# The copy of the last scan states of a chunk, issued on GpSimd instead of ScalarE

## The chip, the cores and the metric

The kernel runs on one core of a Trainium2 chip. The metric is the device time of one execution in microseconds (us); lower is better. Five engines work side by side on a core, each with an instruction queue that it works through in order: TensorE (PE, its weight loads shown apart as PEld), VectorE (DVE), ScalarE (ACT), GpSimd (POOL) and the DMA queue of SyncE (SP).

## The reference, cut to what matters

The input is x, 8 sequences of 1024 tokens with 256 features. The model is a "macaron" layer: half a feed-forward block, a Mamba block, half a feed-forward block, each added to x.

```python
x = x + 0.5 * ffn(layernorm(x))          # fp4 quantise and dequantise, 704 hidden features
x = x + mamba(layernorm(x))              # 512 inner channels, 16 states a channel
x = x + 0.5 * ffn(layernorm(x))

# inside mamba
dA  = jnp.exp(delta[..., None] * A)
dBu = delta[..., None] * Bm[:, :, None, :] * u[..., None]
def step(h, inp):
    dA_t, dBu_t, c_t = inp
    h = dA_t * h + dBu_t
    return h, jnp.einsum('bdn,bn->bd', h, c_t)
```

The part that the change touches is the scan: h runs along the 1024 tokens of a sequence, for each of 512 channels and 16 states, and each h is multiplied by C of its token and summed over the 16 states.

## The kernel before, in words

The tokens are cut into 16 chunks of 512; a sequence is two chunks, so every odd chunk continues an even one. Counting from 0, the even chunks 0, 2, ... 14 begin a sequence and the odd ones end it. Each chunk passes five stages: the first feed-forward block (`stage_f1`), the front of Mamba (`stage_m1`: norm, projections, convolution, delta), the gate (`stage_z`), the scan (`scan`), and the output with the second feed-forward block (`stage_out`). While one chunk is scanned, the feed-forward work of its neighbours is woven in, so all engines always have work of several stages.

The scan of a chunk runs over 16 states k. For each k, `scan_step` makes four tiles s_bu (L874, ACT: delta times u times B, 128 tokens by 512 channels), and then, for each of four groups dc of 128 channels: s_da = exp(delta A) (L878, ACT), four transposes of s_bu into a PSUM tile s_pb (L881, PE; two such buffers), and the scan along the 512 tokens (L883, DVE), which writes a quarter of the tile s_h (five buffers, shared with other tiles of that size). s_h is laid out as two halves a, each of 512 tokens by two channel groups. In an even chunk L908 then copies the last token's 4 values a partition into s_carry, which the odd chunk's scans of the same k read as their initial value, 16 states and some 140 us later. `times_c` (L888) multiplies s_h in place by C, in two products of 1024 elements a partition on POOL. Because it works in place, the first product has to come after the copy of L908 has read s_h. At last the product is added into DRAM by a DMA with an adding write, issued by POOL (L920), or for k = 15 the two DRAM accumulators are added onto s_h (L914, L915), which `stage_out` takes up as y (L852, POOL).

POOL also does the products of the quantisation (`quant`, L543, L545, L552), the Mamba product of L803, and small products of the norm (L610, L613). ACT also does all copies out of PSUM, tanh, squares, the norm's scale and shift.

The order of instructions in each engine's queue is not the program's order. `set_order` (L386) builds a graph of all instructions, gives each a price (`price`, L141) and each pair of engines a lag (`LAG`, L99), plans a list schedule forward and backward in 70 passes, plays the 16 best with random delays, and fixes the winner's order on each engine by ordering dependencies. A small operation on ACT is priced at 93 ns and its elements at 1/1.2 ns each (L158); a copy on POOL falls to the last line of `price` (L177), 176 ns and 1 ns an element. When any instruction changes its engine or price, the whole plan is made anew and the order can move anywhere in the program.

`BE` (L42) chooses a share of the s_bu tiles for VectorE; with `BE = (0,)` the condition of L871 is never true, and all s_bu tiles are made at L874. `CE` (L43) is not used.

Of the kernel before, what the change touches and what calls it, by code (L numbers as in the profile page):

```python
# [14 lines left out]
AF = mybir.ActivationFunctionType  # L15
ALU = mybir.AluOpType
# [21 lines left out]
KS = 1  # L38
KE = 1
W_T = ((0.01, 0.08, 0.085), (0.02, 0.09, 0.095), (0.15, 0.25, 0.3), 0.2)  # L40

BE = (0,)  # L42
CE = (0,)  # L43
BUFS = {
    'accd': 4, 'bcol': 2, 'big': 1, 'bu': 7, 'carry': 2, 'cbc': 2, 'cd': 4, 'da': 4, 'delta': 2,
    'duT': 4, 'h': 5, 'h2': 4, 'hnT': 2, 'ht': 1, 'mv': 4, 'ncar': 2, 'qm': 2, 'qr': 3, 'qs': 4,
# [381 lines left out]
def macaron(ctx: ExitStack, tc: tile.TileContext, x_in, norm_w, norm_b, in_w, conv_w,  # L428
            conv_b, xp_w, dt_w, dt_b, a_log, d_par, out_w, w_gate, w_up, w_down, out):
    nc = tc.nc  # L430
    NB, L, _ = x_in.shape
    chunks = []
    for b in range(NB):
        t = 0
# [3 lines left out]
    S = len(chunks)  # L438
# [90 lines left out]
    def pairs(h, n):  # L529

        return h.rearrange("p (a t q) -> p a t q", a=ND // 2, q=2)[:, :, :n, :]
# [166 lines left out]
    duT, delta, bcol = {}, {}, {}  # L698
    carry = {}
# [132 lines left out]
    def load_y(s):  # L832
        y = pairs(sb.tile([P, ND * T], F32, tag="big", bufs=BUFS["big"], name="o_y"), chunks[s][2])
        yf = y.rearrange("p a t q -> p a (t q)")
        nc.sync.dma_start(yf, accd[s][0])
        nc.gpsimd.dma_start(yf, accd[s][1], accum_op=ALU.add)
        return y
# [25 lines left out]
    def scan_step(s, k, h):  # L863
        n = chunks[s][2]
        nt = n // P
        first = chunks[s][1] == 0
        bu_v = BE[S - 1 - s] if S - 1 - s < len(BE) else 0
        bu = []
        for t in range(nt):
            b = sb.tile([P, DI], F32, tag="bu", bufs=BUFS["bu"], name="s_bu")  # L870
            if t * bu_v % nt < bu_v:  # L871
                nc.vector.tensor_scalar(b, duT[s][t], bcol[s][:, t, k : k + 1], None, ALU.mult)
            else:
                nc.scalar.activation(b, duT[s][t], AF.Copy, scale=bcol[s][:, t, k : k + 1])  # L874
            bu.append(b)
        for dc in range(ND):
            da = sb.tile([P, T], F32, tag="da", bufs=BUFS["da"], name="s_da")[:, :n]
            nc.scalar.activation(da, delta[s][dc], AF.Exp, scale=an[:, dc, k : k + 1])  # L878
            pb = psb.tile([P, T], F32, tag="psb", name="s_pb")[:, :n]
            for t in range(nt):  # L880
                nc.tensor.transpose(pb[:, t * P : (t + 1) * P], bu[t][:, dc * P : (dc + 1) * P], ident)  # L881
            init = 0.0 if first else carry[chunks[s][0]][:, k, dc : dc + 1]
            nc.vector.tensor_tensor_scan(h[:, dc // 2, :, dc % 2], da, pb, init, ALU.mult, ALU.add)  # L883

    def times_c(s, k, h, cbc):
        last = s >= S - KE and k >= NS - 2
        for a in range(ND // 2):
            (nc.vector if last and a else nc.gpsimd).tensor_tensor(  # L888
                h[:, a], h[:, a], cbc.unsqueeze(2).to_broadcast([P, chunks[s][2], 2]), ALU.mult)

    def scan(s):
        n = chunks[s][2]
        if chunks[s][1] == 0:

            carry[chunks[s][0]] = sb.tile([P, NS, ND], F32, tag="carry", bufs=BUFS["carry"], name="s_carry")
        for k in range(0, NS, 2):
            cbc = sb.tile([P, 2, T], F32, tag="cbc", bufs=BUFS["cbc"], name="s_cbc")[:, :, :n]
            nc.sync.dma_start(cbc, cd[s][0:1, k * n : (k + 2) * n].rearrange("o (a t) -> o a t", a=2)
                              .partition_broadcast(P))
            if s >= S - KE and k == NS - 2:  # L900
                y_of[s] = load_y(s)
            last = s >= S - KE and k == NS - 2
            for j in range(2):
                h = pairs(sb.tile([P, ND * T], F32, tag="h", bufs=BUFS["h"], name="s_h"), n)
                hf = h.rearrange("p a t q -> p a (t q)")
                scan_step(s, k + j, h)
                if chunks[s][1] + n < L:
                    nc.scalar.activation(carry[chunks[s][0]][:, k + j].rearrange("p (a q) -> p a q", q=2), h[:, :, n - 1, :], AF.Copy)  # L908
                times_c(s, k + j, h, cbc[:, j, :])
                if last:  # L910
                    last_h.setdefault(s, []).append(h)
                elif k + j == NS - 1:

                    nc.gpsimd.dma_start(hf, accd[s][1], accum_op=ALU.add)  # L914
                    nc.gpsimd.dma_start(hf, accd[s][0], accum_op=ALU.add)  # L915
                    y_of[s] = h
                elif k + j == 1:
                    nc.sync.dma_start(accd[s][1], hf)
                else:
                    nc.gpsimd.dma_start(accd[s][j], hf, accum_op=ALU.add)  # L920
                yield
# [13 lines left out]
    for s in range(S):  # L935
        d = chunks[s][2] / T
        pf, pm = (16, 11) if d == 1 else (9, 9)
        f0 = FIRST[s][0] if s < len(FIRST) else t0 + T_F
        m0 = FIRST[s][1] if s < len(FIRST) else max(t0 + T_M, m1)
        m1 = t0 - E_M if s < len(FIRST) else m0 + d * (t0 - E_M - m0)  # L940
        spread(stage_f1(s), f0, min(f0 + d, m0), pf, K_F if s < KS else 0)
        spread(stage_m1(s), m0, m1, pm, K_M if s < KS else 2)
        spread(stage_z(s), t0 + T_Z, t0 + T_Z + 0.5 * d, ND, 3)
        spread(scan(s), t0, t0 + d, NS)
        t0 += d
        spread(stage_out(s), t0 + T_O, t0 + T_O + d, pf + 3, K_O if s >= S - KE else 1)
# [32 lines left out]
```

## Time and profile before

| | before |
|---|---|
| time of 3 runs, us | 2448.34, 2451.12, 2452.19 (median 2451.12) |
| profiled execution: its time | 2451.14 us |
| profiled execution: its span in the trace | 2449.0 us |
| mean granted TensorE clock | 0.99 |
| the first scan starts, that of chunk 15 starts | 149.5 us, 2261.7 us |
| L908 copies on ACT | 128, 25.9 us of recorded duration, 202 ns mean |

The page of the profile has the busy time of each engine over the span, the span in 40 slices, the DMA queues, the chain of work that ended last followed back from the last instruction, and the costliest groups of instructions with the idle time of the engine before them and what ended it. Other views of the same trace are used: the busy time in stretches of the span, here cut where the scan of a chunk starts, the list of waits (engine and line that waited, what released it, microseconds in total, times, longest), and the timeline of one engine. In the timeline a line has its start, its duration, engine, line of the kernel, operation, tiles out<-in, shape, and in brackets the idle time ahead of it and what ended it.

### The profile page before, as it was taken

How to read it: one execution, taken by the hardware profiler on the slowest of the kernel's cores; microseconds unless marked ns; L12 is line 12 of the kernel's file. 1: busy time of each engine (PE TensorE's matmuls, PEld its weight loads, DVE VectorE, ACT ScalarE, POOL GpSimd, SP SyncE). 2: the span in 40 equal slices, each digit the busy share in tenths (PEclk: the TensorE clock that was granted, in tenths of full speed). 3: DMA queues.
4: the chain of work that ended last, by engine and by line, in shares of the span. 5: the costliest groups of instructions: out<-in, count | busy, mean ns of one | idle time of the engine just before them, and what ended most of it. 6: DMA issues, size and time to landing. Idle time of an engine off the chain costs nothing.

```text
span 2449.0 us, 33713 instructions
## 1 busy us (share of the span) xinstructions
PE 2341.7 (96%) x11260; PEld 1617.9 (66%) x11260; DVE 2177.9 (89%) x3074; ACT 2142.2 (87%) x3952; POOL 2064.2 (84%) x1554
## 2 busy tenths in 40 slices
PE   7989999999999999999999999999999999998888
PEld 5566666667676666666667666666667666655556
DVE  7569898998989899898999889898998989888995
ACT  4489898999989998998999899898998999999852
POOL 4358898899989999898897999899898999888972
PEclk8999999999999999999999999999999999999899
DMA  3049888787877888598886978889787888899970
GB/s 94 18 115 192 192 166 197 166 200 170 165 191 168 203 185 187 138 185 193 175 196 140 210 169 171 189 173 208 167 178 174 179 190 191 189 211 199 198 149 18
DMA packets 90461, 416.28 MB, mean 170 GB/s; under 512 B 12016, under 2 KB 30320, under 8 KB 53552
## 3 DMA queue, kind: packets, MB, share of 16 engines
q0 software_dynamic: 36576, 266.35, 57.6%
q1 hardware_dynamic: 53712, 147.78, 18.4%
q8 instruction: 88, 1.44, 0.2%
q14 instruction: 85, 0.70, 0.1%
HBM read 129.42 MB, written 284.69 MB: 169 GB/s over the span
## 4 chain that ended last, share of the span: by engine, by line
PE 59%; ACT 13%; POOL 11%; DVE 8%; issue 4%; DMA 3%; SPq 0%; POOLq 0%; DVEq 0%; ACTq 0%
PE s_pb L881 11%; PE f_po L662 9%; PE f_pg L642 9%; PE f_pu L642 8%; PE m_pc L765 6%; POOL s_h L888 5%; DVE s_h L883 4%; ACT s_bu L874 4%; PE m_px L755 3%; ACT s_da L878 3%; PE m_pz L823 3%; PE o_po L857 2%; PE m_pp L775 2%; PE m_pd L791 2%; DMA s_h<-accd 2%
## 5 line engine op out<-in xcount | busy, mean ns | idle before, releaser
L888 POOL TENSOR_TENSOR s_h<-s_h,s_cbc 128x1024 f32<-128x1024 f32 x510 | 1136.9, 2270 | 125.0 <-ACT s_carry L908 71.0
L878 ACT ACTIVATE s_da<-m_delta,an 128x512 f32<-128x512 f32 x1024 | 720.7, 718 | 35.3 <-DVE s_h L883 33.5
L881 PEld LDWEIGHTS s_pb<-ident,s_bu 128*128 128x128 f32 x4096 | 505.3, 142 | 335.6 <-issue 132.5
L874 ACT ACTIVATE s_bu<-m_duT,m_bc 128x512 f32<-128x512 f32 x1024 | 701.4, 717 | 12.5 <-PE s_pb L881 9.9
L881 PE MATMUL s_pb<-ident,s_bu 128*128 128x128 f32 x4096 | 652.3, 277 | 44.7 <-DVE s_h L883 34.4
L883 DVE TENSOR_TENSOR_SCAN s_h<-s_da,s_carry,s_pb 128x512 f32<-128x512 f32 x512 | 638.3, 1264 | 22.2 <-PE s_pb L881 18.9
L883 DVE TENSOR_TENSOR_SCAN s_h<-s_da,s_pb 128x512 f32<-128x512 f32 x512 | 608.5, 1206 | 27.3 <-PE s_pb L881 20.2
L662 PE MATMUL f_po<-wdn,f_ht 128*128 128x256 f32 x1536 | 395.3, 382 | 10.0 <-ACT f_ht L659 7.8
L642 PE MATMUL f_pg<-wg,f_xt 128*128 128x352 f32 x1024 | 365.4, 465 | 4.4 <-ACT f_xt L632 1.8
L642 PE MATMUL f_pu<-wu,f_xt 128*128 128x352 f32 x1024 | 360.3, 463 | 5.2 <-DVE f_h L646 3.2
L662 PEld LDWEIGHTS f_po<-wdn,f_ht 128*128 128x128 f32 x1536 | 270.0, 190 | 76.2 <-issue 22.7
L765 PE MATMUL m_pc<-m_xp,cdg 128*128 128x512 f32 x512 | 253.4, 596 | 1.9 <-ACT m_car L762 1.8
L552 POOL TENSOR_TENSOR f_h<-f_h,q_sc 128x704 f32<-128x704 f32 x128 | 195.9, 1534 | 50.8 <-DVE f_h L551 46.2
L642 PEld LDWEIGHTS f_pu<-wu,f_xt 128*128 128x128 f32 x1024 | 177.6, 191 | 89.5 <-issue 21.7
L920 POOL DMA_DIRECT2D accd<-s_h x223 | 209.6, 940 | 26.3 <-POOL s_h L888 18.0
L642 PEld LDWEIGHTS f_pg<-wg,f_xt 128*128 128x128 f32 x1024 | 176.0, 191 | 80.7 <-issue 21.1
L545 POOL TENSOR_TENSOR f_h<-f_h,q_rc 128x704 f32<-128x704 f32 x120 | 176.5, 1479 | 17.0 <-DVE q_rc L544 10.3
L646 DVE SCALAR_TENSOR_TENSOR f_h<-f_h,f_pg 128x352 f32<-128x352 f32 x256 | 129.0, 505 | 37.6 <-ACT f_h L645 36.5
L645 ACT ACTIVATE f_h<-f_pg 128x352 f32<-128x352 f32 x256 | 116.9, 457 | 48.0 <-PE f_pg L642 47.5
L543 POOL TENSOR_SCALAR q_sc<-q_mx 128x44 f32<-128x44 f32 (+2 forms) x198 | 85.5, 439 | 74.2 <-DVE q_mx L542 66.8
L647 DVE TENSOR_TENSOR f_h<-f_h,f_pu 128x352 f32<-128x352 f32 x256 | 129.3, 506 | 18.7 <-PE f_pu L642 17.2
L755 PE MATMUL m_px<-m_hnT,inw 128*128 128x512 f32 x256 | 128.0, 606 | 3.0 <-DVE m_u L769 1.7
(114 smaller groups left out, 3384.6 us busy)
## 6 DMA issues: line engine op xcount, KB each, us to landing
accd<-s_h POOLq DMA_DIRECT2D x223, 1024.0 KB, 9.6
s_cbc<-cd SPq DMA_DIRECT2D x128, 512.0 KB, 6.0
s_h<-accd POOLq DMA_DIRECT2D x30, 1024.0 KB, 8.5
accd<-m_ud SPq DMA_DIRECT2D x16, 1024.0 KB, 13.1
accd<-s_h SPq DMA_DIRECT2D x16, 1024.0 KB, 5.8
x4a<-_attn_hidden_states_dram SPq DMA_DIRECT2D x16, 512.0 KB, 4.3
x1d<-x4a SPq DMA_DIRECT2D x16, 512.0 KB, 6.5
x4b<-x1d SPq DMA_DIRECT2D x16, 512.0 KB, 3.5
```

Source lines behind the costliest of these rows:

```text
L545: mul0.tensor_tensor(vb, vb, rc.unsqueeze(2).to_broadcast([P, g, BLK]), ALU.mult)
L552: mul1.tensor_tensor(vb, vb, sc.unsqueeze(2).to_broadcast([P, g, BLK]), ALU.mult)
L642: nc.tensor.matmul(dst, xt[:, c, :], w[:, c, hf * FH : (hf + 1) * FH], start=(c == 0), stop=(c == 1))
L662: nc.tensor.matmul(po, ht[:, k, :], wdn[:, k, :], start=(k == 0), stop=(k == NF - 1))
L755: nc.tensor.matmul(px, inw[:, c, dc * P : (dc + 1) * P], hnT[:, c, :n], start=(c == 0), stop=(c == 1))
L765: nc.tensor.matmul(pc, cdg[:, dc, k, :], xp[:, k : k + n], start=(k == 0), stop=(k == KC - 1))
L874: nc.scalar.activation(b, duT[s][t], AF.Copy, scale=bcol[s][:, t, k : k + 1])
L878: nc.scalar.activation(da, delta[s][dc], AF.Exp, scale=an[:, dc, k : k + 1])
L881: nc.tensor.transpose(pb[:, t * P : (t + 1) * P], bu[t][:, dc * P : (dc + 1) * P], ident)
L883: nc.vector.tensor_tensor_scan(h[:, dc // 2, :, dc % 2], da, pb, init, ALU.mult, ALU.add)
L888: (nc.vector if last and a else nc.gpsimd).tensor_tensor(h[:, a], h[:, a], cbc.unsqueeze(2).to_broadcast([P, chunks[s][2], 2]), ALU.mult)
L920: nc.gpsimd.dma_start(accd[s][j], hf, accum_op=ALU.add)
```

## The change

GpSimd now issues the copy of L908, as a `tensor_copy`, at the same place in the program: after the four scans of a state and ahead of the two products. The number of copies, their source and their destination are the same. The knobs `BE` and `CE` are removed, with the branch that `BE = (0,)` never took. The plan of all queues is made anew, with the copy priced as a POOL instruction.

```diff
-BE = (0,)
-CE = (0,)
...
-        bu_v = BE[S - 1 - s] if S - 1 - s < len(BE) else 0
         bu = []
         for t in range(nt):
             b = sb.tile([P, DI], F32, tag="bu", bufs=BUFS["bu"], name="s_bu")
-            if t * bu_v % nt < bu_v:
-                nc.vector.tensor_scalar(b, duT[s][t], bcol[s][:, t, k : k + 1], None, ALU.mult)
-            else:
-                nc.scalar.activation(b, duT[s][t], AF.Copy, scale=bcol[s][:, t, k : k + 1])
+            nc.scalar.activation(b, duT[s][t], AF.Copy, scale=bcol[s][:, t, k : k + 1])
             bu.append(b)
...
                 if chunks[s][1] + n < L:
-                    nc.scalar.activation(carry[chunks[s][0]][:, k + j].rearrange("p (a q) -> p a q", q=2), h[:, :, n - 1, :], AF.Copy)
+                    nc.gpsimd.tensor_copy(carry[chunks[s][0]][:, k + j].rearrange("p (a q) -> p a q", q=2), h[:, :, n - 1, :])
                 times_c(s, k + j, h, cbc[:, j, :])
```

## The prediction

> **What bounds the kernel now.** I read the page's busy shares first, then the stretches by chunk, then the waits. The stretches are cut where a chunk's scan starts (even chunks begin at 149.5, 427.8, 714.0, ...). The columns are the stretch, its length, and the busy time of PE, PEld, DVE, ACT and POOL with instruction counts, then granted clock, DMA share and GB/s.
>
> ```profile
> 149.50:278.90 129.40, 120.02 (x564) 78.82 (x562) 111.87 (x148) 123.16 (x232) 109.40 (x78) 0.96 0.87 191
> 278.90:427.80 148.90, 143.92 (x683) 99.43 (x683) 138.20 (x200) 133.41 (x240) 134.80 (x103) 0.98 0.83 178
> 427.80:569.20 141.40, 138.61 (x678) 96.81 (x678) 131.00 (x190) 132.05 (x250) 126.54 (x94) 1.00 0.81 180
> 714.00:851.50 137.50, 135.62 (x662) 93.94 (x661) 129.05 (x187) 128.81 (x247) 125.22 (x93) 1.00 0.80 180
> 1863.50:2000.60 137.10, 136.09 (x669) 95.72 (x668) 128.15 (x184) 130.31 (x250) 125.94 (x94) 1.00 0.81 184
> 2131.70:2261.70 130.00, 116.92 (x546) 76.00 (x546) 106.53 (x130) 120.93 (x223) 111.60 (x76) 0.99 0.92 205
> ```
>
> The reader is to see two kinds of stretch. In the middle (four of the lines) PE is busy for all but 1 to 5 us of 137 to 149; those stretches are PE's, and nothing in the change touches PE's work. In chunk 0 (first line) and chunk 14 (last line) PE idles 9.4 and 13.1 us, and ACT is the fullest engine (idle 6.2 and 9.1). These are where the copies on ACT could set the time. The head (0 to 149.5) and chunk 15 (2261.7 to the end) hold no copy.
>
> POOL idles 11 to 20 us in every stretch with copies, ACT 6 to 13. The waits say for what:
>
> ```profile
> PEld s_pb L881 <- DVE s_h L883: 95.8, 207, 1.8
> POOL s_h L888 <- ACT s_carry L908: 71.0, 53, 8.0
> ...
> POOL s_h L888 <- DVE s_h L883: 48.8, 67, 2.1
> ...
> PEld s_pb L881 <- ACT s_bu L874: 25.6, 51, 1.9
> ```
>
> POOL's longest wait is for the copy, 71.0 us in 53 pieces. But in the odd chunks, which have no copy, it waits for the scan itself (48.8 us in 67): most of the 71 us is the scan being awaited, under another name. And who waits for the products? In the list for line L888 only the DMA issue of L920 does (20.2 us, 59 times), never PE or DVE. A product earlier or later by half a microsecond reaches PE only through POOL's other work.
>
> **What the change removes: 128 copies on ACT.** Their rows show 202 ns each, 25.9 us. That is not what ACT gets back, since records overlap:
>
> ```profile
> 153.25 1.32 ACT L878 ACTIVATE s_da<-m_delta,an 128x512 f32<-128x512 f32 x2
> 154.48 0.19 ACT L908 ACTIVATE s_carry<-s_h 128x4 f32<-128x4 f32 x1
> 154.57 0.70 ACT L874 ACTIVATE s_bu<-m_duT,m_bc 128x512 f32<-128x512 f32 x1
> ```
>
> The next instruction starts 0.09 us after the copy; the median over the 114 copies with ACT busy on both sides is 95 ns. So ACT gets 128 x 0.095 = 12.2 us, 1.5 us an even chunk, plus the 2.6 us for which it stood waiting for a scan ahead of a copy.
>
> **What it adds: 128 copies on POOL.** The trace has no POOL copy. Bounds from the nearest rows: below, the 3-element MEMSET of L758, 40 ns (median end to end behind a busy POOL); above, the 32-element TENSOR_SCALAR of L543, 0.32 us. Nearest in shape and in reading two small operands from SBUF is L613 (128x4), behind its producer on POOL:
>
> ```profile
> 1310.06 1.03 POOL L610 TENSOR_TENSOR bn_y<-bn_ve,mhalf 128x4 f32<-128x4 f32 x1 [0.98 <-ACT bn_ve L609]
> 1311.17 0.20 POOL L613 TENSOR_TENSOR bn_nm<-bn_m,bn_y 128x4 f32<-128x4 f32 x1
> ```
>
> It takes 0.20 us, and a dependent instruction starts 0.08 us after its producer's end (1310.06 + 1.03 = 1311.09 to 1311.17). I take 0.20 + 0.08 = 0.28 us a state: 128 x 0.28 = 36 us on POOL, 4.5 us an even chunk, with ends 0.04 x 128 = 5 us and (0.32 + 0.08) x 128 = 51 us.
>
> **What it moves: a wait.** Before, the way was scan, ACT's queue, copy, POOL. Over the 128 copies of the trace the copy starts a mean 0.65 us after the last scan's end, takes 0.20, and the product follows 0.08 us later when POOL was idle: 0.93 us, at best 0.03 + 0.20 + 0.08 = 0.31. After, POOL starts 0.08 us after the scan (the commonest distance in the odd chunks where POOL waited), copies for 0.20 and begins the product 0.08 later: 0.36 us. Where POOL now waits, it gains some 0.4 us on average (ends: a loss of 0.05, a gain of 2). Summed over the copies behind which POOL sat idle, taking from each its own distance from scan to product beyond 0.41 (0.36 and 0.05 to be careful), or its idle time where that is shorter, the gain is 20 us. So POOL pays 36 and gets back about 20: 16 us net, 2 us an even chunk, against 11 to 20 us idle there. Behind the waiting copy on POOL stand the quantiser's products (L545, L552), for which PE and ACT do wait; but the in-place product held the same place before and waited longer. No DMA is moved; the issues of L920 follow the product as before. The copied values are read a chunk later, so nothing waits for them. The removed BE branch was never taken: nothing.
>
> A rule that speaks against the change: the Trainium skill (GPSIMD Engine Reference, "Performance versus the Vector engine") has a software dispatch on GpSimd in two hops for each instruction and calls the engine the wrong choice for ordinary elementwise work. The trace agrees as far as it goes: 0.15 to 0.20 us for L613 on POOL against 0.095 on ACT. By the rule alone the move would be a loss of 36 - 12 = 24 us of engine time; it is not, in the sum here, because neither engine sets the middle stretches.
>
> **The sum.** Chunks 0 and 14, where ACT is fullest: 2 x 1.5 = 3.0 us off (bounds: 0, and the 2 x 3.2 us of the copies' recorded durations). The six even chunks between: PE idles there 2.8 + 1.9 + 3.7 + 5.3 + 1.5 + 1.0 = 16.2 us in all, mostly ahead of s_pb; ACT's 1.5 us is some 15% of its 6.8 to 13.3 us idle, and I let PE's idle shrink by that share: 2.4 us (bounds 0 and 16). POOL's 2 us net an even chunk is under its idle time; without that cover it would be 16 us. I charge 0.4. Sum -5.0. The profiled execution took 2451.14 us (span 2449.0, 2.1 around it), the median of the runs is 2451.12: 2446.
>
> **The new plan.** All queues are planned anew. What an order is worth by chance I estimate from equal work in the present order: chunk pairs 2+3 to 10+11 last 286.2, 286.5, 289.2, 288.6 and 285.2 us, a standard deviation of 1.7 a pair; over 8 pairs 1.7 times the root of 8, 4.8, and with the head and the tail, planned by the same means, I take 8 us either way.
>
> **The rivals.**
>
> *Nothing moves: 2451.* For: PE at 97 to 99% in the middle, and POOL's wait changing only its name, from L908 on ACT to the scan. Against: chunks 0 and 14, which are not PE's.
>
> *POOL becomes late: 2465.* If a POOL copy costs the upper 0.40 us and POOL seldom waits for ACT in the new order, POOL pays 51 and saves 20: 31 us, 4 us an even chunk. It decides from the point where POOL's idle time is all forced by scans and quantiser steps (in chunk 4 its idle is 12 us, mostly that), so the quantiser's products come late, and with them f_xn and f_h for the transposes on PE, at L552 to L630. Half of 31 on the path less 2 for ACT gives +14. For: PE already waits for POOL at L630 (13.9 us for PEld, 8.4 for PE). Against: POOL's idle time is the largest of the four in chunk 0 and in chunk 14 except for DVE's.
>
> *ACT's queue is worth more than its time: 2434.* If copies that wait in ACT's queue hold back s_da and s_bu, PE's 25.6 us of waits for L874 and DVE's chain behind it shrink: two thirds of the 25.6 gives -17. Against: ACT waited for a scan ahead of a copy 2.6 us only.
>
> *An unlucky order:* the sum holds, and the plan adds 8 or more: 2454 to 2460.
>
> **How the numbers follow.** About 0.2% (4.9 us) is what a measurement of this kernel can tell from no change. Small gain as summed 0.35; ACT worth more 0.15; nothing moves 0.20; POOL late 0.17; unlucky order 0.13. The small gain with its plan lies on the edge: some 0.30 of its 0.35 I count as faster, 0.05 as the same. Faster 0.45, same 0.25, slower 0.30. Range 2430 (the ACT case with a good order) to 2469 (POOL late with a few us of bad order); the likeliest case alone 2438 to 2454.
>
> **What would show it.** POOL busy up by 20 to 40 us, ACT down by 26 recorded; a POOL row at L908's successor of about 0.2 us; the 71.0 us wait gone and a wait of the POOL copy for DVE s_h of about 45 to 55 in its place; chunks 0 and 14 shorter by 1 to 3 us each, the middle pairs equal within 3. Wrong if the POOL copy takes over 0.4 us; if the middle pairs move together by over 3 us; if PE's waits at L630 grow (POOL late); or if the difference lies in the head or chunk 15, which have no copy: then it is the plan.

## The result and the profile after

The changed kernel takes 2478.18 us (median of 4 runs, 2475.19 to 2483.46); the kernel before, beside it, 2450.26. The ratio is 1.0116 (95% interval 1.0096 to 1.0137): slower by some 28 us, outside the predicted range of 2430 to 2469. The profiled execution took 2480.05 us, its span is 2478.3.

The page of the changed kernel, its first lines and three groups (line L901 is the copy, L881 the product, L876 the scan; all lines behind the removed code stand 3 to 7 lower):

```profile
span 2478.3 us, 33729 instructions
...
PE 2347.7 (95%) x11260; PEld 1622.5 (65%) x11260; DVE 2178.0 (88%) x3074; ACT 2134.9 (86%) x3824; POOL 2084.0 (84%) x1682
...
L881 POOL TENSOR_TENSOR s_h<-s_h,s_cbc 128x1024 f32<-128x1024 f32 x510 | 1123.5, 2236 | 66.3 <-DVE s_h L876 52.5
```

All of PE's work is there as before, and PE idles 23 us more: 2478.3 - 2347.7 = 130.6 us against 2449.0 - 2341.7 = 107.3. Summed over the list of waits, PE's waits that DVE ended grew from 45.8 to 68.8 us, while those that ACT and POOL ended stayed at 53 to 54 together. The other 6 us are recorded PE time, beside a slightly lower granted clock (0.985 against 0.99). Of these, 4.0 lie in chunk 15 with the end of the program, first before and then after (columns as in the prediction):

```profile
2261.70:2449.00 187.30, 157.72 (x785) 114.23 (x783) 150.38 (x198) 109.97 (x191) 115.40 (x86) 0.96 0.56 121
```

```profile
2285.60:2478.30 192.70, 161.71 (x774) 117.81 (x771) 150.36 (x196) 108.89 (x191) 114.15 (x86) 0.91 0.55 118
```

POOL's busy time grew by 20 us, ACT's fell by 7.

The waits of the changed kernel, those that answer to the lines of before:

```profile
PEld s_pb L874 <- DVE s_h L876: 102.8, 212, 2.2
...
POOL s_h L881 <- DVE s_h L876: 52.5, 70, 2.1
...
POOL s_carry L901 <- DVE s_h L876: 38.2, 30, 8.0
...
PEld s_pb L874 <- ACT s_bu L867: 21.0, 41, 1.4
```

The wait for ACT's copy (71.0 us) is gone and 38.2 us of it have come back under POOL's own copy. So the wait that the change is about moved as forecast. The time went elsewhere. By pairs of chunks, cut where the even chunk's scan starts (the table is worked out from the stretches of both traces):

| stretch | before, us | after, us | difference | PE idle before | after |
|---|---|---|---|---|---|
| chunks 0+1 | 278.3 | 286.2 | +7.9 | 14.4 | 18.6 |
| 2+3 | 286.2 | 288.6 | +2.4 | 4.1 | 9.3 |
| 4+5 | 286.5 | 297.5 | +11.0 | 3.9 | 9.6 |
| 6+7 | 289.2 | 288.5 | -0.7 | 5.8 | 7.6 |
| 8+9 | 288.6 | 289.4 | +0.8 | 7.9 | 6.6 |
| 10+11 | 285.2 | 284.5 | -0.7 | 4.0 | 5.3 |
| 12+13 | 268.2 | 272.0 | +3.8 | 3.4 | 6.1 |
| 14 to the end | 317.3 | 322.5 | +5.2 | 42.7 | 46.4 |

The lines behind the largest difference, chunks 4 and 5, before and after:

```profile
714.00:1000.50 286.50, 282.56 (x1372) 196.09 (x1371) 266.23 (x379) 265.18 (x490) 258.24 (x192) 1.00 0.81 180
```

```profile
723.90:1021.40 297.50, 287.86 (x1387) 199.04 (x1386) 267.01 (x381) 267.64 (x481) 262.02 (x210) 0.99 0.79 174
```

Every even chunk has the same 16 copies, yet one pair loses 11 us and others nothing. That is a hint, not a proof, that the copy itself is not what costs: a copy can also cost more in one chunk than in another. It pointed to the other half of the change: every queue had been ordered anew.

### The profile page after: what moved, and what is told of

It is laid out like the page before. It is cut to its first block, busy times and chain, and to the rows that moved or that the text cites. A ratio compares the mean times of both kernels' runs of the same rounds, so it can differ in the third digit from the quotient of the medians.

```text
span 2478.3 us, 33729 instructions
## 1 busy us (share of the span) xinstructions
PE 2347.7 (95%) x11260; PEld 1622.5 (65%) x11260; DVE 2178.0 (88%) x3074; ACT 2134.9 (86%) x3824; POOL 2084.0 (84%) x1682
## 3 DMA queue, kind: packets, MB, share of 16 engines
q1 hardware_dynamic: 53712, 147.78, 18.2%
## 5 line engine op out<-in xcount | busy, mean ns | idle before, releaser
L881 POOL TENSOR_TENSOR s_h<-s_h,s_cbc 128x1024 f32<-128x1024 f32 x510 | 1123.5, 2236 | 66.3 <-DVE s_h L876 52.5
L874 PE MATMUL s_pb<-ident,s_bu 128*128 128x128 f32 x4096 | 647.3, 278 | 47.5 <-DVE s_h L876 42.7
L876 DVE TENSOR_TENSOR_SCAN s_h<-s_da,s_carry,s_pb 128x512 f32<-128x512 f32 x512 | 639.1, 1263 | 18.4 <-PE s_pb L874 15.0
L876 DVE TENSOR_TENSOR_SCAN s_h<-s_da,s_pb 128x512 f32<-128x512 f32 x512 | 607.9, 1205 | 21.5 <-PE s_pb L874 16.5
L542 POOL TENSOR_TENSOR f_h<-f_h,q_rc 128x704 f32<-128x704 f32 x120 | 170.6, 1434 | 19.5 <-DVE q_rc L541 13.8
L643 DVE SCALAR_TENSOR_TENSOR f_h<-f_h,f_pg 128x352 f32<-128x352 f32 x256 | 129.4, 506 | 56.4 <-ACT f_h L642 55.2
L642 ACT ACTIVATE f_h<-f_pg 128x352 f32<-128x352 f32 x256 | 116.8, 457 | 46.6 <-PE f_pg L639 45.3
L547 DVE SCALAR_TENSOR_TENSOR f_h<-q_q,f_h 128x704 f32<-128x704 f32 x128 | 112.3, 877 | 28.0 <-ACT q_q L546 27.7
## 6 DMA issues: line engine op xcount, KB each, us to landing
accd<-m_ud SPq DMA_DIRECT2D x16, 1024.0 KB, 11.6
```

The source lines that it names most:

```text
L542: mul0.tensor_tensor(vb, vb, rc.unsqueeze(2).to_broadcast([P, g, BLK]), ALU.mult)
L643: nc.vector.scalar_tensor_tensor(hh, hh, 1.0, pg, ALU.add, ALU.mult)
L881: (nc.vector if last and a else nc.gpsimd).tensor_tensor(h[:, a], h[:, a], cbc.unsqueeze(2).to_broadcast([P, chunks[s][2], 2]), ALU.mult)
```

## The experiments

Two theories stood at the start. *Order*: the loss is that of the newly planned order of all queues; the engine that copies matters little. *Engine*: the loss is GpSimd's time in 128 copies, or its wait.

### Order and engine apart: e1 and e2

The plan is made as if the copies were on the one engine, and they are then issued on the other. The graph gets the wanted engine and price, and the queues are filled by the instruction's own engine. For e1 (base: the kernel before) each copy is put directly ahead of its first product in POOL's queue:

```diff
+    if carries(i):
+        return (4 / 1.2 + 93, 0, 0, False)
...
-        self.eng = [i.engine for i in insts]
+        self.eng = [ET.Activation if carries(i) else i.engine for i in insts]
...
+        if c is not None and c not in placed and insts[x].engine == ET.Pool:
+            seqs[ET.Pool].append(c)
...
-                    nc.scalar.activation(carry..., h[:, :, n - 1, :], AF.Copy)
+                    nc.gpsimd.tensor_copy(carry..., h[:, :, n - 1, :])
```

e2 is the reverse on the changed kernel: planned with POOL's price, issued on ACT at the planned place. Apart from the copies, PE, DVE, SP and the rest of ACT and POOL have the order of before in e1, and of the changed kernel in e2.

> The copies run on GpSimd, each directly ahead of its product, but every other instruction keeps the order of the kernel before on its engine. If the new order made the loss (order theory): within 0.3% of before, 2443 to 2458 us. If the work or the wait on GpSimd made it (engine theory): like the changed kernel, 2470 to 2485. Half of each: about 2464.

> The copies run on ScalarE, but the order is the one planned for the changed kernel (planned as if they were on GpSimd). Order theory: like the changed kernel, 2470 to 2485 us, perhaps some us more, since the order was not made for copies on ScalarE. Engine theory: like before, 2443 to 2458.

Measured: e1 2457.78 us, ratio 1.0028 (1.0017 to 1.0040). e2 2478.11 us, ratio 1.0115 (1.0101 to 1.0129).

| | copies on ScalarE | copies on GpSimd |
|---|---|---|
| order of before | 2450 | 2458 |
| order of the changed kernel | 2478 | 2478 |

The order makes 20 to 28 of the 28 us. The engine makes 8 in the order that was planned for ScalarE, and none in the order planned for GpSimd. The 8 are known to some 3: the interval of e1's ratio is 4 to 10 us. In e1's profiled execution, 7.8 us longer than that of before, 3.3 lie in chunk 15 with the end, which has no copy (PE is busy there for 163.1 us at a granted clock of 0.93, against 157.7 at 0.96). The stretches tell order and engine apart in the same way. Chunks 4 and 5 together, in e1 and then in e2 (columns as in the prediction):

```profile
714.00:1001.00 287.00, 282.83 (x1372) 195.95 (x1371) 266.14 (x379) 264.10 (x474) 261.19 (x208) 1.00 0.81 180
```

```profile
723.60:1019.00 295.40, 287.20 (x1388) 198.21 (x1386) 267.27 (x380) 269.30 (x497) 259.37 (x194) 1.00 0.79 176
```

With the order of before the pair takes 287.0 us with copies on POOL (286.5 with ACT); with the new order 295.4 with copies on ACT (297.5 with POOL). PE's single stalls sit at the same instruction too. PE's timeline of the changed kernel, and then of e2:

```profile
565.00 0.38 PE L655 MATMUL f_pb<-ident,f_h 128*128 128x128 f32 x2
566.79 0.86 PE L639 MATMUL f_pg<-wg,f_xt 128*128 128x352 f32 x2 [1.41 <-DVE f_h L643]
```

```profile
564.60 0.38 PE L655 MATMUL f_pb<-ident,f_h 128*128 128x128 f32 x2
566.38 0.86 PE L639 MATMUL f_pg<-wg,f_xt 128*128 128x352 f32 x2 [1.41 <-DVE f_h L643]
```

A stall of 1.41 us ahead of the same matmul, whichever engine copies. It comes back at 863.2, 1151.5 and 1441.9 us of the changed kernel, so it stands once in each of the four pairs from 2+3 to 8+9.

### Is the order of before a lucky one? e3 to e7, e14, e15

If a new order costs 28 us, what is an ordinary order worth? Seven kernels change nothing on the chip but the plan. Six shift the five weights with which the planner starts, three with copies on ScalarE and three on GpSimd; e7 raises the planner's price of ScalarE's copy by 1 ns.

```diff
-WEIGHTS = (0.05, 0.1, 0.15, 0.2, 0.3)
+WEIGHTS = (0.06, 0.11, 0.16, 0.21, 0.31)     # e3, e4; all lowered by 0.01: e5, e6; raised by 0.02: e14, e15
...
+    if carries(i):                             # e7
+        return (4 / 1.2 + 94, 0, 0, False)
```

> The kernel before, with the five path weights of the planner raised by 0.01: copies on ScalarE, another order. Order theory with the order of before as a lucky one: slower than before, 2455 to 2490 us. Engine theory: within 8 us of before, whatever the order.

> The changed kernel, with the same five weights raised by 0.01: copies on GpSimd, another order. Order theory: anywhere between 2450 and 2490 us, no nearer to the changed kernel than the redrawn kernel before is. Engine theory: within 8 us of 2478 and 20 to 36 us above the redrawn kernel before.

> The kernel before, copies on ScalarE; only the planner's price of the copy is raised by 1 ns. Order theory, with the order of before as one lucky draw: a new order and 2455 to 2490 us. Engine theory: 2445 to 2456, as nothing on the chip's engines is changed.

> The kernel before with the planner's five path weights lowered by 0.01: copies on ScalarE, another draw of the order. Order theory: somewhere in 2455 to 2485 us, as the draws so far (2460, 2479); a third draw at or under 2451 would say that the order of before is an ordinary one.

> The changed kernel with the same weights lowered by 0.01: copies on GpSimd, another draw. If the engine matters beside the order by the 8.5 us of the held order: 2465 to 2490 us, above the draws with copies on ScalarE by some 8. If the order alone matters: 2455 to 2485.

> The kernel before with the five path weights raised by 0.02, a fourth draw with copies on ScalarE (draws so far 2460, 2467, 2479). Lucky order: 2455 to 2485 us again. Ordinary order: at or under 2452.

> The changed kernel with the weights raised by 0.02, a fourth order with copies on GpSimd (so far 2461, 2478, 2479). If the engine costs 8 us beside the order: 2463 to 2490 us. If only the order counts: 2455 to 2485, and not above the draw with copies on ScalarE.

| order drawn by | copies on ScalarE | copies on GpSimd |
|---|---|---|
| the kernels as given | 2450 (before) | 2478 (changed) |
| weights + 0.01 | 2479.35 (e3), 1.0117 (1.0104 to 1.0131) | 2478.69 (e4), 1.0112 (1.0096 to 1.0127) |
| weights - 0.01 | 2466.72 (e5), 1.0060 (1.0048 to 1.0072) | 2460.64 (e6), 1.0044 (1.0028 to 1.0059) |
| weights + 0.02 | 2474.62 (e14), 1.0100 (1.0084 to 1.0115) | 2472.26 (e15), 1.0087 (1.0073 to 1.0100) |
| price + 1 ns | 2459.67 (e7), 1.0040 (1.0028 to 1.0053) | |

One nanosecond in the price of 128 instructions moves the time by 9 us. The four redraws on ScalarE have a mean of 2470.1 us and a standard deviation of 9; the four orders on GpSimd 2472.4 and 8. The groups do not differ by more than the draws' own error (2.3 us, with 6 for the difference of two such means): whether orders with copies on GpSimd are slower as a group stays open below that. The kernel before lies 21 us under the mean of the eight and 9 under the best of them. It is a lucky order, and an edit that makes the planner draw again loses that luck on average. Shifted weights could also plan worse by themselves, which no run rules out; e7 leaves them alone and loses 9 us. Whether the order of before was once picked for its time is not on record.

### What the copy itself costs in a held order: e8, e9, e11, e13

All four keep the order of before, as e1 does. e8 issues each POOL copy twice; e11 each ACT copy twice; e9 lets POOL's copy read a constant tile, so that it waits for no scan; e13 lets 128 small DMAs of SyncE fill the tile, so that no compute engine copies (in e9 and e13 the odd chunks start from other values).

```diff
# e8 (e11 the same with nc.scalar.activation)
+                    for _ in range(2): nc.gpsimd.tensor_copy(carry..., h[:, :, n - 1, :])
# e9 (e13 with nc.sync.dma_start)
+                    nc.gpsimd.tensor_copy(carry..., an[:, :, 0].rearrange("p (a q) -> p a q", q=2))
```

> Order of the kernel before; each copy runs twice in a row on GpSimd ahead of its product (the second writes the same values again). The single copy in this order cost 8.5 us. If that is GpSimd's time in the copy (hold theory), a second one adds again about as much: 2463 to 2470 us. If it is the wait ahead of the copy (wait theory), the second adds little: 2455 to 2460.

> Order of the kernel before; the copy on GpSimd at its place ahead of the product reads a constant tile in place of the last states, so it waits for no scan (the carried states are then not the scan's; the odd chunks start from other values). Hold theory: as the single copy, 2454 to 2460 us. Wait theory: 2444 to 2451, as before or better by ScalarE's 12 us of work.

> Order of the kernel before; copies on ScalarE, each twice in a row (the second writes the same values again). It prices ScalarE's time from the other side: if ScalarE's 12 us of copies are worth what the prediction took for them, about 5 us, the second set adds 4 to 9: 2454 to 2460 us. If ScalarE's time is covered: 2448 to 2453.

> Order of the kernel before; neither ScalarE nor GpSimd has the copies: 128 small DMAs of SyncE fill the carried states from a constant tile (so they are not the scan's), and the products wait for their scans alone. If ScalarE's 12 us of copies were on the path by the share that its doubling showed (11.6 us for 31 us added, 0.37): 2444 to 2448 us. If taking work from ScalarE gives nothing while adding costs: 2449 to 2453. If it is worth all it takes: 2437 to 2441.

Measured: e8 2472.45 us, 1.0091 (1.0077 to 1.0105); e9 2451.99, 1.0004 (0.9995 to 1.0013); e11 2462.72, 1.0050 (1.0038 to 1.0062); e13 2457.24, 1.0024 (1.0014 to 1.0033).

How POOL pays is read from its timeline, at the same copy in e1, e8 and e9:

```profile
792.00 0.19 POOL L908 COPY s_carry<-s_h 128x4 f32<-128x4 f32 x1
792.27 2.14 POOL L888 TENSOR_TENSOR s_h<-s_h,s_cbc 128x1024 f32<-128x1024 f32 x1
```

```profile
796.24 0.44 POOL L908 COPY s_carry<-s_h 128x4 f32<-128x4 f32 x2
796.76 2.13 POOL L888 TENSOR_TENSOR s_h<-s_h,s_cbc 128x1024 f32<-128x1024 f32 x1
```

```profile
790.27 0.19 POOL L908 COPY s_carry<-an 128x4 f32<-128x4 f32 x1
790.43 2.14 POOL L888 TENSOR_TENSOR s_h<-s_h,s_cbc 128x1024 f32<-128x1024 f32 x1
```

From the copy's start to the product's start: 0.27 us for one, 0.52 for two, 0.16 where the product need not wait for the copy's end. This is the price behind an idle POOL. Behind a busy one the copy costs more. The order is the same in before and e1, so each product can be set beside itself: in the 63 of 128 places where POOL is busy ahead of it in both, the product starts 0.43 us later on average, counted from the start of the same instruction ahead. Most of the 63 lie near 0.25 (23 are under 0.35) or between 0.46 and 0.61 (33). In before the product often starts ahead of the recorded end of that instruction; behind a copy it starts 0.08 us after the copy's end.

The second copy of e8 adds 0.25 x 128 = 32 us to POOL. Against the kernel before run beside each, e8 takes 21.7 us more and e1 8.5, so these 32 us add some 13: about 40% reaches the end. The way is seen at L630, where PE waits for POOL's f_xn: 8.4 us in before, 9.0 in e1 and 14.1 in e8, and for PEld 13.9, 16.9 and 23.2. The same on ACT: in e11 the second copy waits for the first, and the pair holds ACT for a median of 0.34 us in place of 0.095, 31 us more; the time grows by 11.6. Neither engine's idle time covers all of what is added.

Of the two theories of the expectations neither holds alone. e8 lies above the range of the hold theory, so a second copy is far from free; e9 lies at the range of the wait theory (2451.99 against 2444 to 2451), so a copy that need not follow the scan costs little. In the 64 places where POOL is busy in both, e9's product comes a median of 0.13 us later than in before.

In the other direction little or nothing comes back. e9 frees ACT of 12 us and has POOL's copy partly in the shadow of the wait for the scan, and is equal to before within its interval. It bounds the relief and does not show it to be nothing: its POOL copies, at most 0.16 x 128 = 20 us, could at e8's rate hide up to 8 us of it. e13 frees ACT and burdens no compute engine, and is 6 us slower. Its stretches show why it is no clean measure: against before, the even chunks 0, 2, 8, 10 and 14 differ by -0.5 to +0.3 us, while chunks 4, 6 and 12 lose 2.0, 4.5 and 1.4. In chunk 6 DVE waits 3.1 us for the load of x4c, which it does not in before; the small DMAs stand in the same queue of SyncE. That they hold up that load is argued, not shown. The five stretches that lost nothing put ACT's relief at some 0.3 us a stretch, of the 1.5 taken off ACT; they were chosen after the result, so this is a hint.

### Copies on VectorE: e10 and e12

A third engine, again in the order of before: the copy directly behind the last of the four scans in DVE's queue.

```diff
+                    nc.vector.tensor_copy(carry..., h[:, :, n - 1, :])                                    # e10
+                    nc.vector.tensor_reduce(carry..., h[:, :, n - 1, :].unsqueeze(3), AX.X, ALU.max)      # e12
```

> Order of the kernel before; the copies run on VectorE directly behind the last of their four scans, so neither ScalarE nor GpSimd has them. If the 8.5 us are GpSimd's time or wait: 2443 to 2450 us. If any engine pays the same for 128 small instructions, since PE waits for VectorE's scans more than for anything else: 2455 to 2462.

> Order of the kernel before; the copies on VectorE behind the last scan, but as a maximum over an axis of one element in place of a copy. If the 53 us of the copy on VectorE came from its waiting for GpSimd's running products (31 of 128 copies took over 0.4 us, 50 us together): 2447 to 2457 us. If they came from VectorE's place in the chain of scans: 2490 to 2505 again.

e10 took 2504.12 us, 1.0216 (1.0200 to 1.0233), 53 us more than before: neither expectation. The group of the copy in e10, then in e12 (mean in ns behind the busy time):

```profile
L908 DVE COPY s_carry<-s_h 128x4 f32<-128x4 f32 x128 | 67.6, 528 | 4.4
```

```profile
L908 DVE TENSOR_REDUCE s_carry<-s_h 128x4 f32<-128x4 f32 x128 | 20.1, 157 | 4.4
```

Four elements a partition, and the copy takes a mean of 528 ns; the shortest is 169 and 31 of the 128 take over 0.4 us, 50 us together. One of these on DVE's timeline, and below it POOL's timeline of the same microseconds:

```profile
1045.64 3.79 DVE L908 COPY s_carry<-s_h 128x4 f32<-128x4 f32 x1
1049.34 1.21 DVE L883 TENSOR_TENSOR_SCAN s_h<-s_da,s_pb 128x512 f32<-128x512 f32 x1
```

```profile
1044.63 1.34 POOL L552 TENSOR_TENSOR f_xn<-f_xn,q_sc 128x512 f32<-128x512 f32 x1
1045.65 2.40 POOL L888 TENSOR_TENSOR s_h<-s_h,s_cbc 128x1024 f32<-128x1024 f32 x1
1047.74 1.64 POOL L552 TENSOR_TENSOR f_h<-f_h,q_sc 128x704 f32<-128x704 f32 x1
```

The copy ends at 1049.43, 0.05 us behind the end of POOL's third product (1047.74 + 1.64 = 1049.38). All 31 long copies end within 0.1 us of the end of a POOL product. The Trainium skill (Perfetto Trace Analysis, "Optimizing Scalar/DVE Operations") says that the two engines share a port which a DVE instruction in its fast two-port mode holds as an exclusive lock; these rows agree, from the side of the DVE instruction that has to get the lock. That the copy runs in this mode, and the maximum of e12 does not, no run here shows by itself. e12 does the same work as a maximum over one element, which takes 157 to 163 ns each time and never waits: 2455.05 us, 1.0018 (1.0010 to 1.0027). So 49 of the 53 us were the copy's waiting. Set beside the same place of before, the maximum puts the next DVE instruction back by a median of 0.19 us, 25 us in all; the time grows by 4, with ACT freed of its 12.

### Where in the order the loss sits: e16 and e17

The stall of 1.41 us above has a place. The timeline of all engines there in the changed kernel:

```profile
564.43 1.28 ACT L642 ACT_TABLE_LOAD   x1
...
565.72 0.46 ACT L642 ACTIVATE f_h<-f_pg 128x352 f32<-128x352 f32 x1
...
566.22 0.52 DVE L643 SCALAR_TENSOR_TENSOR f_h<-f_h,f_pg 128x352 f32<-128x352 f32 x1 [2.64 <-ACT f_h L642]
```

Each chunk's softplus needs another function table on ACT; the first tanh or exponential behind it loads the old one again, 1.28 us. In the changed order that is a feed-forward tanh (L642) in 10 of 15 chunks: PE waits for DVE, DVE for the tanh, the tanh for the table. In before it is a tanh of the gate (the line that is L826 there) in 12 of 15, with 3 at the feed-forward one. The groups of before, then of the changed kernel:

```profile
L826 ACT ACT_TABLE_LOAD x12 | 15.4, 1283 | 0.2
...
L645 ACT ACT_TABLE_LOAD x3 | 3.8, 1283 | 0.1
```

```profile
L642 ACT ACT_TABLE_LOAD x10 | 12.8, 1283 | 0.2
...
L823 ACT ACT_TABLE_LOAD x5 | 6.4, 1283 | 0.1
```

PE's idle time within 3.5 us of a load's start, from 150 us on, is 6.7 us in before, 14.9 in the changed kernel and 15.0 in e2; over the redraws, from the fastest to the slowest, it tends to grow with the time, with e15 as the exception (e7 12.2, e6 12.0, e5 12.0, e15 10.6, e14 18.2, e4 18.1, e3 19.5). That the load stands at the feed-forward tanh is not the whole of it: e14, e4 and e3, with the most idle time, have it there in only 4 or 5 chunks. To test the loads' share, both orders are run with an exponential in place of the softplus, which needs no other table (delta has other values then); the planner's price is kept for it, and so is the order.

```diff
-        nc.scalar.activation(dl, dl, AF.Softplus)
+        nc.scalar.activation(dl, dl, AF.Exp)
...
-        return (hold + 2720, -1310, 0, False) if "Softplus" in str(i.func) else (hold, 0, 0, False)
+        return (hold + 2720, -1310, 0, False) if "Exp" in str(i.func) and n == 2048 else (hold, 0, 0, False)
```

> Order of the kernel before, with an exponential in place of the softplus of delta (so delta, and all behind it, is another value): the function table of ScalarE is then loaded once, not twice a chunk (30 loads of 1.28 us less after the head). Reload theory (the orders differ in how well they cover the second load: PE idles 6.7 us within 3.5 us of a load here and 14.9 in the changed kernel): 5 to 10 us under before, 2441 to 2446, and the distance to the changed order without reloads falls from 28 to about 20 us. Spread theory (the loss of the order has no such place): the distance stays 26 to 30 us.

> The changed kernel in its own order, with the same exponential in place of the softplus (delta has other values) and so without the reloads. Reload theory: 13 to 20 us under the changed kernel, 2458 to 2465, and about 20 us above the same edit in the order of before. Spread theory: 26 to 30 us above that.

e16 took 2451.62 us, 1.0005 (0.9996 to 1.0014); e17 2468.87, 1.0072 (1.0059 to 1.0084). The distance of the two orders falls from 28 to 17 us, as the reload theory has it, so some 10 us of the order's loss are its poorer cover for the reloads. The ranges of the times were missed: e17 gained 9 us where 13 to 20 were expected, and taking 38 us of loads away from before gained nothing where 5 to 10 were expected. So the order of before covers its loads; the 6.7 us of idle time near them must then have other causes, which were not looked for. The remaining 17 us are spread over the stretches (in e17, chunks 1, 4 and 13 lose 4.9, 8.0 and 8.1 us against before and chunk 15 with the end 5.5, others up to 3 either way), and no one place was found.

## Why the prediction was wrong, point by point

**What bounds the kernel.** Right in the middle stretches: PE is busy for all but a few us there, and PE's idle time is what grew. Wrong in the conclusion that POOL's added time is therefore covered: some 40% of what e8 added to POOL reached the end.

**The new plan: the step that failed.** The prediction took "8 us either way", from how little five pairs of one order differ. Above all it centred the draw on the present order, as if that were an average one; the redraws put the mean 21 us above it. The term was 0 +- 8; it measured +28 on ScalarE's copies and +20 on GpSimd's. The five pairs also said little of the scatter: their standard deviation, 1.7 us in before, is 4.8 in the changed kernel and 0.5 in e14. That the pairs of an order are not independent draws, since the planner repeats its weaving, is only argued: the 1.41 us stall stands in four pairs, and two of these lose nothing by the table.

**What ACT gets back: mis-sized.** The prediction took off 3.0 us in chunks 0 and 14 and 2.4 in the others. The time of e9 shows no gain, and the five stretches of e13 that lost nothing give 0.3 us each. Chunk 0 is 131.5 us long after and 129.4 before; chunk 14 129.8 and 130.0. In the held order they are shorter by 0.2 and 1.9 us (e9) and by 0.3 and 0.5 (e13), of the 1.5 each that were forecast. That ACT is the fullest engine of a stretch was not enough to make it the one that sets it.

**What POOL pays: the price right behind an idle POOL only, the cover wrong.** 0.28 us was predicted and 0.27 is seen behind an idle POOL; behind a busy one it is 0.43 on average, above the 0.40 of the upper end. The wait that POOL saves was also misread: 0.65 us from the scan's end to ACT's copy is near the median over the 128 copies (0.68), and their mean is 1.32. And the 0.4 us charged for POOL measured 8.5 (e1); e8 shows the rate: some 40% of POOL's added time reaches the end, although POOL idles 11 to 20 us a stretch. A share of the busy time says nothing of the slack of each instruction; POOL's idle pieces lie where it waits for others, and PE waits for f_xn behind POOL's products (L630, above).

**The rivals.** "POOL becomes late" had the mechanism of e1 and e8, with its waits at L630, and gave it 14 us; 8.5 came in the order of before, and nothing in the changed order. "An unlucky order" had the right cause for most of the loss, at 0.13 and at 8 us: the chance and the size were both too low. "ACT's queue is worth more" forecast -17 us; e9, equal to before with at most 8 us hidden, leaves no room for that in the order of before. The copy wait of 45 to 55 us on POOL was 38.2; POOL's busy time grew by 20 of the 20 to 40; ACT's fell by 7 and not by 26. The records overlap, as the prediction had found (0.095 of 0.202 us, 12 us in all); why it is 7 and not 12 stays open. The prediction's last test was that a difference in the head or in chunk 15, which have no copy, would mean the plan. Chunk 15 with the end grew from 187.3 to 192.7 us, but that is no clean sign: 4.0 of it is PE time at a lower granted clock, and e1, with the order of before, has 190.6 us there. Chunk 1, also without copies, is the better sign: it grew from 148.9 to 154.7 us, and lasts 147.8 to 148.7 in the held-order runs.

## What to carry to other kernels

Where a program fixes the order of its queues by a search, an edit that touches any price is two changes: itself, and a new draw. Hold the order to measure the first, and redraw both versions several times to size the second, before either is believed; here the draws scatter by some 9 us and the kernel before was the best of nine. In the one order where it was measured, relief was worth little and additions were dear: work taken off ACT gave no gain that could be seen, and about 40% of what was added to POOL or ACT reached the end, though POOL idles for 16% of the time and ACT for 13%.

## What the runs showed of the hardware that was not expected

A VectorE copy of 128x4 from SBUF to SBUF took up to 4.60 us (median 170 ns) while GpSimd products ran, and made the kernel 2.2% slower; the same four values through a one-element maximum took 157 to 163 ns each time. On GpSimd a 128x4 copy behind an idle engine takes 0.18 to 0.19 us; from its start to the next instruction's start it is 0.16 us ahead of an independent product and 0.27 ahead of one that depends on it. Behind a busy GpSimd it put the dependent product back by 0.43 us on average. On ScalarE a second write to the same four elements behind the first made the pair hold the engine 0.34 us, where a single copy holds it 0.095.
